# An eight-batch attention kernel: the last batch's scores are taken further ahead, and its last probabilities are turned a step sooner

## The chip, the core and the metric

The kernel runs on one core of a Trainium2 chip. The metric is device time in microseconds of one execution. Before the change it is 431.56 us, the median of three runs (429.86 to 432.5). PE is TensorE, DVE VectorE, ACT ScalarE, POOL GpSimd; SP issues transfers.

## What is computed

For each of 8 batches, 112 queries attend with 20 heads of 16 channels to 371 text tokens; four further prompt tokens have keys and values of their own, and their logits get half the cosine between the attended text and the prompt token. In the reference, cut to what matters:

```python
q = heads(hidden_states @ W_q)
k_t, v_t = heads(text_ehs @ W_k), heads(text_ehs @ W_v)
probs_t = softmax(einsum('bhsd,bhtd->bhst', q, k_t) * attn_scale)
text_out = einsum('bhst,bhtd->bhsd', probs_t, v_t)
attn_scores = einsum('bhsd,bhnd->bhsn', q, k_ip) * attn_scale
qsem = _l2norm(einsum('bhst,bte->bhse', probs_t, text_ehs))
sem = einsum('bhse,bne->bhsn', qsem, _l2norm(ip_ehs))
probs_ip = softmax(attn_scores + 0.5 * sem) * spatial_mask
out = (text_out + einsum('bhsn,bhnd->bhsd', probs_ip, v_ip)) @ W_out + b_out + residual
```

The length of the attended text is never formed from its 512 channels: with the Gram matrix G of the tokens it is the square root of p G p, so each head needs the product of its probabilities with G, the values and the prompt columns, and then a sum of that product times the probabilities.

## The kernel before

**Tiling.** The 20 heads of a batch are five groups of four. One step (b, g), counted from zero, handles one group of one batch; there are 40 steps. The four heads of a group lie on four bands of 32 partitions, so four small matmuls run side by side.

**A group's way.** `scores` (L672 to L689) multiplies masked queries and keys into one PSUM bank for each head. `probabilities` (L691 to L710) takes the maximum on DVE (L695), the exponential on ACT (L699), copies the four prompt logits (L701), and sends the probabilities by SP into `xg`, a ring of two buffers (L708). `transposed` (L712) turns `xg` on DVE into `xgT`, of which there are two (in the last batch in two halves). `multiplied` (L724) makes 48 matmuls, in 12 rounds of four with shrinking width (392 columns down to 40, 2592 over a head's twelve), into four banks (L737). Then the bank is evacuated: values and prompt products to `pvs` (L750, or L767), and the sum of product times probability either in one DVE instruction (L785, "junk") or, for some heads of the last steps, by `shared`: a copy on ACT (L768), a product on POOL (L772), a sum on ACT (L778). `placed` (L644) has POOL write the group's values into the right operand `u` (L651), chunk by chunk. `finish` (L802 to L924) ends a batch: squares and a maximum (L826, L828), a root and a table load on ACT (L843, L844), a reciprocal and the prompt softmax on DVE (L850 to L868), the prompt sums and the output projection on PE.

**Stores.** PSUM has eight banks: four `qd`, two `sc`, two `mm`; `bank(name, spare)` gives an `sc` or an `mm` bank. Probabilities have three buffers (`p`).

**Order.** On PE, SP and DVE, and from the second batch on ACT too, the instructions stand in the order in which the program calls them; in the last batch that holds for POOL too. So each engine is a queue written out by hand. In the main loop (L1187) a step issues the scores of the group two steps on: two of them at the first round and two at the seventh; the first two's probabilities follow at once, the others' after the step. At the third round the next group is turned. After the step come value copies, reductions, the placing of the next values, and in `between` (L1070) projections for later batches: keys, values, queries. `project_queries` (L315) runs in pieces; the last query product of batch 7 (L340) stands between (6,4) and (7,0).

**The last batch (L1260).** The same look-ahead of two steps: scores of group 2 in (7,0), of group 3 partly before and partly in (7,1), of group 4 in (7,2). The last third of the keys (`last_keys`, L550) stands between (7,0) and (7,1), in a `qd` bank, in two halves with two scores between. `finish` of batch 6 is threaded through the steps. The third transfer of group 4 is issued from ACT's queue (L710). Group 4 is turned in (7,3). `shared` takes three heads of groups 0, 1 and 2 and one of group 3. After the steps comes a tail in which batch 6 and batch 7 are finished.

Of the kernel before, what the change touches and what calls it, by code (L numbers as in the profile page):

```python
# [8 lines left out]
F32 = mybir.dt.float32  # L9
AF = mybir.ActivationFunctionType  # L10
# [10 lines left out]
def kernel(  # L21
# [292 lines left out]

    def project_queries(bs):  # L315
        n = len(bs)
        xT = work.tile([P, NC, 2 * S], F32, tag="xT", name=f"xT_{bs[0]}", bufs=1)
        qm = work.tile([P, NC, 2, 2 * S], F32, tag="qm", name=f"qm_{bs[0]}", bufs=2)

        qT = const.tile([P, NC, S], F32, tag="qT", name="qT") if bs[0] == 0 else None  # L320
        for j, b in enumerate(bs):
            queries[b] = (qT, qm, j)
        nc.gpsimd.memset(xT[REST:, FULL, :], 0.0)
        for i in range(NC):
            cn = min(P, C - i * P)
            if bs[0] == 0:

                ps = ps_qd.tile([P, 512], F32, tag="qd", name=f"ps_x_0_{i}")
            else:
                ps = bank(f"ps_x_{bs[0]}_{i}", spare=i > 0)  # L330
            for j, b in enumerate(bs):
                nc.tensor.transpose(
                    ps[:cn, j * S : (j + 1) * S], x_sb[:, b, i * P : i * P + cn], ident[:S, :S]
                )
            nc.scalar.copy(xT[:cn, i, : n * S], ps[:cn, : n * S])
            yield
        for i in range(NC):
            ps = bank(f"ps_q_{bs[0]}_{i}")
            for j in range(NC):
                nc.tensor.matmul(  # L340
                    ps[:, : n * S],
                    wq_sb[:, j, i * P : (i + 1) * P],
                    xT[:, j, : n * S],
                    start=(j == 0),
                    stop=(j == NC - 1),
                )

            for r in range(2 if i < FULL else 1):
                nc.vector.tensor_scalar_mul(  # L349
                    qm[:, i, r, : n * S], ps[:, : n * S], emask[:, r : r + 1]  # L350
                )
            if qT is not None:
                nc.scalar.copy(qT[:, i, :], ps[:, :S])
            yield
# [333 lines left out]
        )  # L688
        s["sc", g, a] = ps  # L689

    def probabilities(b, g, a):  # L691
# [3 lines left out]
        nc.vector.tensor_reduce(nmx, ps[:S, :TT], AX.X, ALU.max, negate=True)  # L695
        if ("p", g) not in s:
            s["p", g] = work.tile([S, GROUP, TT], F32, tag="p", name=f"p_{b}_{g}", bufs=3)
        p = s["p", g][:, a, :]
        nc.scalar.activation(p, ps[:S, :TT], AF.Exp, bias=nmx)  # L699
        if b > 0:  # L700
            nc.scalar.copy(s["ipl"][:, groups[g][a], :], ps[:S, TT:T])  # L701

        xg = x_ring[(b * NG + g) % NX]
        rows = xg[a * RG : a * RG + S // QN, :, :TT]
        if (b, g, a) == (B - 1, NG - 1, 1):
            s["third"] = rows, p
            return
        nc.sync.dma_start(rows, p)  # L708
        if "third" in s:
            nc.scalar.dma_start(*s.pop("third"))  # L710

    def transposed(b, g):  # L712

# [10 lines left out]
    def multiplied(b, g):  # L724
        s = st[b]
        xT = s.pop(("xT", g))
        banks = []
        for a in range(GROUP):

            if b == B - 1 and g % 2 and g < NG - 1:  # L730
                banks.append(bank(f"ps_qd_{b}_{g}_{a}", spare=a > 1))
            else:
                banks.append(ps_qd.tile([P, 512], F32, tag="qd", name=f"ps_qd_{b}_{g}_{a}"))
        for j in range(BLK):
            c, q = PLACE[j] if b > 0 else (j // QN, j % QN)
            for a in range(GROUP):
                nc.tensor.matmul(  # L737
                    banks[a][:S, j * RG : UW],
                    xT[a * RG : (a + 1) * RG, j, :S],
                    region(b, c)[a * RG : (a + 1) * RG, q, j * RG - c * P :],  # L740
                    start=(j == 0),
                    stop=(j == BLK - 1),
                )
            yield
        s["qd", g] = banks
# [6 lines left out]
    def shared(b, g, n):  # L752
# [17 lines left out]

        for a, _ in some:
            nc.gpsimd.tensor_tensor(prods[a], prods[a], p[:, a, :], ALU.mult)  # L772
            if (b, g) == (B - 1, LEAD) and a < n - 1:
                yield
        yield

        for a, (h, _) in some:
# [292 lines left out]
    def between(b, g):  # L1070
# [43 lines left out]
        if g == 4:  # L1114
            if b > 0 and new:
                run(("f", b - 1), None, 2)
            if nb < B - 1:
                run(("k", nb), None, 1)
            for bs in (first if b > 0 else []) + rest:
                run(("q", bs[0]), None)  # L1120

    prompts = normalised_prompts()
# [60 lines left out]
            load_x(5, B)  # L1183


    ctx.enter_context(tc.manual_schedule(engines=engines | {mybir.EngineType.Activation}))
    for n, (b, g) in enumerate(steps[:-NG]):  # L1187
        coming = steps[n + LEAD]
# [17 lines left out]
        for a in (0, 1):  # L1206
            probabilities(*coming, a)
        if n == len(steps) - NG - 1:
            sums = shared(b, g, GROUP // 2)
            next(sums)  # L1210
# [36 lines left out]
    b = B - 1  # L1247
    before = ("f", b - 1)

    def coming(g, heads):  # L1250

        for a in heads:
            if g == 1:
                ps = ps_qd.tile([P, 512], F32, tag="qd", name=f"ps_s_{b}_{g + LEAD}_{a}")
            else:
                ps = bank(f"ps_s_{b}_{g + LEAD}_{a}", spare=a > 1)
            scores(b, g + LEAD, a, ps=ps)
            probabilities(b, g + LEAD, a)

    for g in range(NG):  # L1260
        if g == 1:
            keys3 = last_keys(b, ps_qd.tile([P, 512], F32, tag="qd", name=f"ps_k_{b}_{FULL}"))
            next(keys3)
            coming(g, (3, 0))
            next(keys3)
            run(before, lambda: finish(b - 1, bd=bd[:, 0]))
        places = {0: {0: (2, 3), 1: (0, 1)}, 1: {0: (1, 2)}, 2: {0: (3, 0), 1: (1, 2)}}.get(g, {})
        for j, _ in enumerate(multiplied(b, g)):
            coming(g, places.get(j, ()))
            if g == NG - 2 and j in (QN - 1, 2 * QN - 1):  # L1270
                next(sums)
                placed(b, g + 1, (j // QN,))
            if j != 2:
                continue
            if g < LEAD:
                drain(sums)
            if g + 1 < NG:
                transposed(b, g + 1)
            if g == 2:
                run(before, None)  # L1280
            if g == 3:
                run(before, None)
        ahead = sums
        if g < NG - 1:

            n = GROUP - 1 if g <= LEAD else 1
            sums = shared(b, g, n)
            next(sums)
            reduced(b, g, n)
            if g <= LEAD:  # L1290
                value_sums(b, g, n)
            if g == NG - 2:
                placed(b, g + 1, (NT - 1,))
                next(ahead)
            else:
                placed(b, g + 1)
            if g != LEAD:
                next(sums)
        if g == 0:
            own_channels(bd)  # L1300
            with_bias(b)
            run(("f", b - 2), None)
        if g == 2:
            run(before, None, 2)
            drain(ahead)
            nc.scalar.preload_act_table(AF.Sqrt)
        if g == 3:
            drain(ahead)
            drain(sums)
            value_sums(b, g, n)  # L1310

            first = finish(b, (0, FULL * HC), bd=bd[:, 1])
            for _ in range(3):
                next(first)
    value_sums(b, g)
    next(first)
    late = projected_prompts(bd[:, 1])
    run(before, None)
    next(late)
# [62 lines left out]
```

## Time and profile before

| What | us |
|---|---|
| median of three runs | 431.56 |
| the profiled execution | 432.11 |
| its span, first to last instruction | 430.1 |
| PE busy (share) | 418.8 (97%) |
| DVE busy (share) | 326.8 (76%) |
| ACT busy (share) | 190.1 (44%) |
| POOL busy (share) | 111.6 (26%) |
| granted TensorE clock, mean | 1.000 |

The page gives busy time for each engine and the chain of work that ended last. The timeline lists instructions of one engine that follow each other as one row: start, time, engine, line, operation, out<-in, shape, count, and in brackets how long the engine had been idle and what ended that. PEld is the load of the stationary operand, which overlaps PE. In the timeline the four matmuls of a round overlap, so a row's time is longer than the work's share of it. Idle time of an engine that nobody waits for costs nothing.

### The profile page before, as it was taken

The page shows a single profiled execution, that of the slowest core. Times are in us where ns is not written, and L with a number is a line of the kernel's source. Part 1 is how long each engine was busy: PE and PEld are TensorE (multiplying, and loading weights), DVE is VectorE, ACT ScalarE, POOL GpSimd, SP SyncE. Part 2 cuts the span into 40 slices and gives each one's busy share as a digit, 9 for nine tenths or more (in the row PEclk, how much of TensorE's full clock was granted, in tenths as well). Part 3 has the DMA queues.
Part 4 walks back from the last instruction along what each step waited for, and adds up shares of the span by engine and source line. Part 5 has one row for each costly group of instructions (what it writes and reads, how often), then busy time and mean ns, then how long its engine had stood idle before and what let it go on. Part 6 is the DMA issues. An engine that isn't in the chain of part 4 may idle for free. (4 is left out here: it accounts for less than half of the span.)

```text
span 430.1 us, 13979 instructions
## 1 busy us (share of the span) xinstructions
PE 418.8 (97%) x5521; PEld 327.3 (76%) x5521; DVE 326.8 (76%) x670; ACT 190.1 (44%) x662; POOL 111.6 (26%) x276
## 2 busy tenths in 40 slices
PE   8999999989999999999999999999999999999976
PEld 7867768878777877888777977789777887776773
DVE  4038569787887878887897978888878877878784
ACT  2344342345334353435334353344533463346783
POOL 5310101112061212421251111511142120527340
PEclk9999999999999999999999999999999999999999
DMA  8677665687646966576646946477656446553300
GB/s 234 201 192 209 141 167 161 160 200 148 161 127 145 202 155 168 140 164 147 168 121 139 203 117 175 123 163 153 168 139 160 132 109 185 139 127 111 93 2 27
DMA packets 57630, 64.26 MB, mean 149 GB/s; under 512 B 18448, under 2 KB 51592, under 8 KB 57566
## 3 DMA queue, kind: packets, MB, share of 16 engines
q1 hardware_dynamic: 56808, 62.26, 58.2%
q10 hardware_dynamic: 758, 1.13, 0.9%
q8 instruction: 43, 0.70, 0.7%
q14 instruction: 21, 0.17, 0.1%
HBM read 18.67 MB, written 5.32 MB: 56 GB/s over the span
## 5 line engine op out<-in xcount | busy, mean ns | idle before, releaser
L737 PE MATMUL ps_qd<-u,xgT 32*112 32x328 f32 (+11 forms) x3840 | 220.1, 353 | 1.3 <-DVE xgT L718 1.3
L737 PEld LDWEIGHTS ps_qd<-u,xgT 32*112 32x112 f32 x3840 | 187.0, 172 | 34.5 <-issue 10.9
L718 DVE STREAM_TRANSPOSE xgT<-xg 128x1536 f32<-128x1536 f32 (+1 forms) x45 | 119.1, 2667 | 11.4 <-DMA xg<-p 10.8
L699 ACT ACTIVATE p<-ps_s,nmx 112x371 f32<-112x371 f32 x160 | 86.9, 580 | 84.4 <-DVE nmx L695 59.7
L695 DVE TENSOR_REDUCE nmx<-ps_s 112x1 f32<-112x371 f32 x160 | 77.7, 528 | 42.1 <-PE ps_s L682 40.0
L785 DVE CUSTOM_DVE_ANT_0 junk<-ps_qd,p 112x371 f32<-112x371 f32 x148 | 80.2, 542 | 15.5 <-ACT kT L536 0.5
L682 PE MATMUL ps_s<-kT,qm 32*112 32x375 f32 (+1 forms) x320 | 66.8, 485 | 0.7 <-ACT shared L768 0.7
L651 POOL COPY u<-vr 128x64 f32<-128x64 f32 x120 | 26.0, 237 | 149.5 <-PE ps_qd L737 100.2
L574 PE MATMUL ps_v<-wv_sb,ctxT 128*128 128x384 f32 (+1 forms) x192 | 63.6, 480 | 0.0
L574 PEld LDWEIGHTS ps_v<-wv_sb,ctxT 128*128 128x128 f32 x192 | 35.2, 190 | 19.7
L540 PE MATMUL ps_k<-ctxT,wk_sb 128*128 128x371 f32 x136 | 46.3, 483 | 0.2 <-DVE ctxT L421 0.2
L750 ACT COPY pvs<-ps_qd 112x21 f32<-112x21 f32 x150 | 15.9, 188 | 64.0 <-PE ps_qd L737 63.1
L540 PEld LDWEIGHTS ps_k<-ctxT,wk_sb 128*128 128x128 f32 x136 | 24.9, 190 | 15.2 <-POOL ct L138 0.5
L682 PEld LDWEIGHTS ps_s<-kT,qm 32*112 32x112 f32 x320 | 26.8, 170 | 6.8 <-ACT kT L547 2.1
L498 PE MATMUL ps_g<-ctxT 128*32 128x375 f32 (+11 forms) x672 | 30.4, 333 | 0.0
L498 PEld LDWEIGHTS ps_g<-ctxT 128*32 128x32 f32 x672 | 27.7, 110 | 2.0
L701 ACT COPY ipl<-ps_s 112x4 f32<-112x4 f32 x140 | 23.4, 167 | 0.0
L349 DVE TENSOR_SCALAR qm<-ps_q,emask 128x224 f32<-128x224 f32 (+1 forms) x25 | 9.1, 399 | 17.6 <-PE ps_q L340 17.5
L400 DVE STREAM_TRANSPOSE ctxT<-ct 128x512 f32<-128x512 f32 x18 | 20.0, 1109 | 1.9 <-DMA ct<-in_ctx_dram 1.9
L581 ACT COPY vext<-ps_v 128x384 f32<-128x384 f32 (+1 forms) x24 | 11.3, 471 | 21.2 <-PE ps_v L574 21.2
L471 POOL TENSOR_TENSOR ug<-ug,half 128x128 f32<-128x128 f32 (+1 forms) x24 | 10.4, 446 | 32.0 <-ACT ug L470 32.0
L928 POOL TENSOR_TENSOR wv<-vip,w 112x1280 f32<-112x1280 f32 x6 | 14.8, 2465 | 14.2 <-DVE w L868 14.2
(167 smaller groups left out, 320.7 us busy)
## 6 DMA issues: line engine op xcount, KB each, us to landing
xg<-p SPq DMA_DIRECT2D x159, 162.3 KB
u<-ug SPq DMA_DIRECT2D x124, 99.0 KB
ct<-in_ctx_dram SPq DMA_DIRECT2D x24, 176.0 KB
vr<-vd SPq DMA_DIRECT2D x32, 120.0 KB
vip<-vipd SPq DMA_DIRECT2D x6, 560.0 KB
vd<-vext SPq DMA_DIRECT2D x7, 320.0 KB
vd<-vext SPq DMA_DIRECT2D x7, 160.0 KB
out_dram<-ob SPq DMA_DIRECT2D x8, 140.0 KB
```

The costliest lines, as they stand in the source:

```text
L400: nc.vector.transpose(ctxT[:, :, c * P : (c + 1) * P].rearrange("p e (j i) -> p j e i", i=RG), ct[:, some, :].rearrange("p j (k e) -> p j ...
L498: nc.tensor.matmul(ps[c][q * RG : (q + 1) * RG, j * RG - c * P : T - c * P], ctxT[:, e, j * RG : (j + 1) * RG], ctxT[:, e, j * RG : T], st ...
L540: nc.tensor.matmul(ps[:, :TT], wk_sb[:, e, i * P : (i + 1) * P], s["ctxT"][:, e, :TT], start=(e == 0), stop=(e == NE - 1),)
L574: nc.tensor.matmul(ps[:, :w], ctxT[:, e, c * P : (c + 1) * P], wv_sb[:, e, :w], start=(e == 0), stop=(e == NE - 1),)
L651: nc.gpsimd.tensor_copy(v, dealt(b, c, s["vr"][:, c * QN : (c + 1) * QN, g, :]))
L682: nc.tensor.matmul(ps[:S, :w], qm[a * RG : (a + 1) * RG, i, r, j * S : (j + 1) * S], s["kT"][a * RG : (a + 1) * RG, i, :w], start=True, st ...
L695: nc.vector.tensor_reduce(nmx, ps[:S, :TT], AX.X, ALU.max, negate=True)
L699: nc.scalar.activation(p, ps[:S, :TT], AF.Exp, bias=nmx)
L701: nc.scalar.copy(s["ipl"][:, groups[g][a], :], ps[:S, TT:T])
L718: nc.vector.transpose(xT[:, j : j + n].rearrange("p j (k q) -> p q j k", q=QN), xg[:, :, j * RG : (j + n) * RG].rearrange("p q (j k) -> p ...
L737: nc.tensor.matmul(banks[a][:S, j * RG : UW], xT[a * RG : (a + 1) * RG, j, :S], region(b, c)[a * RG : (a + 1) * RG, q, j * RG - c * P :], ...
L785: nc.vector.tensor_tensor_reduce(out=junk, in0=ps[:S, :TT], in1=s["p", g][:, a, :], scale=1.0, scalar=0.0, op0=ALU.mult, op1=ALU.add, accu ...
```

## The change

From step (6,3) on, scores are issued half a group further ahead. `ahead` (new) gives for each step which scores come at its first round, which of them get an `mm` bank and have their transfer held back (`hold`, `sent`), and which come at the seventh round. (6,3) issues all four of (7,0) and two of (7,1); (6,4) the other two of (7,1) and all of (7,2); (7,0) all of group 3; (7,1) all of group 4, at its third and fourth rounds; (7,2) none. Held transfers are issued after the turn that frees their ring buffer. The probabilities of groups 1 and 3 of the last batch get other homes (`home`): a free context buffer and the value weights, which have had their last use. The last query product of batch 7 moves from between (6,4) and (7,0) to between (7,0) and (7,1), behind the last keys, which stand there in one piece and in an `mm` bank. Groups 2, 3 and 4 are turned one step sooner, at the ends of (7,0), (7,1) and (7,2). `shared` takes three, three, two and no heads of groups 0 to 3, and its last sums on ACT come a step later. All of group 4's transfers are on SP. In the tail the weights of batch 6 (L863 to L868) come after the first root's inputs of batch 7.

```diff
@@ project_queries
-            ps = bank(f"ps_q_{bs[0]}_{i}")
+            if end and i == FULL:
+                ps = ps_qd.tile([P, 512], F32, tag="qd", name=f"ps_q_{bs[0]}_{i}")
+            else:
+                ps = bank(f"ps_q_{bs[0]}_{i}")
@@ probabilities
-        if (b, g, a) == (B - 1, NG - 1, 1):
-            s["third"] = rows, p
-            return
-        nc.sync.dma_start(rows, p)
-        if "third" in s:
-            nc.scalar.dma_start(*s.pop("third"))
+        if not hold:
+            sent(b, g, a)
@@ between
-            for bs in (first if b > 0 else []) + rest:
+            for bs in (first if b > 0 else []) + (rest if b < B - 2 else []):
@@ the main loop
+    def ahead(n):
+        c, d = steps[n + LEAD : n + LEAD + 2]
+        if steps[n] == (B - 2, NG - 2):
+            todo = ((c, 2, 3), (c, 0, 1), (d, 2, 3))
+        elif steps[n] == (B - 2, NG - 1):
+            todo = ((c, 0, 1), (d, 2, 3), (d, 0, 1))
+        else:
+            todo = ((c, 2, 3), (c,), (c, 0, 1))
+        return [[(t[0], a) for a in t[1:]] for t in todo]
...
-            for a in {0: (2, 3), 6: (0, 1)}.get(j, ()):
-                scores(*coming, a)
-                if j == 0:
-                    probabilities(*coming, a)
+            if j == 0:
+                for c, a in now:
+                    scores(*c, a)
+                    probabilities(*c, a)
+                for c, a in more:
+                    scores(*c, a, ps=bank(f"ps_s_{c[0]}_{c[1]}_{a}"))
+                    probabilities(*c, a, hold=True)
+            if j == 6:
+                for c, a in then:
+                    scores(*c, a)
             if j == 2:
...
                 transposed(*steps[n + 1])
+                for c, a in more:
+                    sent(*c, a)
@@ the last batch
         if g == 1:
-            keys3 = last_keys(b, ps_qd.tile([P, 512], F32, tag="qd", name=f"ps_k_{b}_{FULL}"))
+            keys3 = last_keys(b, bank(f"ps_k_{b}_{FULL}"))
             next(keys3)
-            coming(g, (3, 0))
             next(keys3)
-            run(before, lambda: finish(b - 1, bd=bd[:, 0]))
+            run(("q", b), None)
+            drain(late)
...
+            if g == 0 and j < 2:
+                for a in ((2, 3), (0, 1))[j]:
+                    coming(NG - 2, a, bank(f"ps_s_{b}_{NG - 2}_{a}", spare=a > 1))
+            if g == 0 and j == 2:
+                transposed(b, 1)
+                for a in range(GROUP):
+                    sent(b, NG - 2, a)
+            if g == 1 and j in (2, 3):
+                for a in ((3, 2), (1, 0))[j - 2]:
+                    ps = ps_qd.tile([P, 512], F32, tag="qd", name=f"ps_s_{b}_{NG - 1}_{a}")
+                    coming(NG - 1, a, ps)
+            if g == 1 and j == 4:
+                run(before, lambda: finish(b - 1, bd=bd[:, 0]))
...
+        n = (3, 3, 2, 0)[g]
+        late, sums = sums, shared(b, g, n) if n else iter(())
+        next(sums, None)
+        reduced(b, g, n)
+        value_sums(b, g, n)
+        if g == LEAD:
+            run(before, None, 2)
+        if 0 < g + 1 < NG - 1:
+            transposed(b, g + 2)
+        placed(b, g + 1, range(NT) if g == 0 else (NT - 1,))
+        next(sums, None)
+        if g > 0:
+            drain(late)
```

More of the change, by code (lines that the diff above doesn't have):

```diff
@@ L316, in project_queries @@
         n = len(bs)
+        end = bs[0] == B - 1
         xT = work.tile([P, NC, 2 * S], F32, tag="xT", name=f"xT_{bs[0]}", bufs=1)
@@ L689, in scores, with home, probabilities @@
         s["sc", g, a] = ps
-    def probabilities(b, g, a):
+    def home(b, g):
+        if b == B - 1 and g == 1:
+            t = io.tile([P, NT, E], F32, tag="ct", name=f"p_{b}_{g}").rearrange("p c e -> p (c e)")
+        elif b == B - 1 and g == 3:
+            t = wv_sb.rearrange("p e f -> p (e f)")
+        else:
+            return work.tile([S, GROUP, TT], F32, tag="p", name=f"p_{b}_{g}", bufs=3)
+        return t[:S, : GROUP * TT].rearrange("p (a t) -> p a t", t=TT)
+    def probabilities(b, g, a, hold=False):
         s = st[b]
@@ L728, in multiplied @@
         for a in range(GROUP):
-            if b == B - 1 and g % 2 and g < NG - 1:
+            if b == B - 1 and g % 2:
                 banks.append(bank(f"ps_qd_{b}_{g}_{a}", spare=a > 1))
@@ L772, in shared @@
             nc.gpsimd.tensor_tensor(prods[a], prods[a], p[:, a, :], ALU.mult)
-            if (b, g) == (B - 1, LEAD) and a < n - 1:
-                yield
         yield
@@ L1183, in load_rest @@
             load_x(5, B)
+    def ahead(n):
[4 more added lines that the diff above has]
+            todo = ((c, 0, 1), (d, 2, 3), (d, 0, 1))
+        else:
+            todo = ((c, 2, 3), (c,), (c, 0, 1))
+        return [[(t[0], a) for a in t[1:]] for t in todo]
     ctx.enter_context(tc.manual_schedule(engines=engines | {mybir.EngineType.Activation}))
     for n, (b, g) in enumerate(steps[:-NG]):
-        coming = steps[n + LEAD]
+        now, more, then = ahead(n)
         for j, _ in enumerate(multiplied(b, g)):
-            for a in {0: (2, 3), 6: (0, 1)}.get(j, ()):
-                scores(*coming, a)
-                if j == 0:
-                    probabilities(*coming, a)
+            if j == 0:
[8 more added lines that the diff above has]
+                    scores(*c, a)
             if j == 2:
@@ L1205 @@
             run(("f", b - 1), None)
-        for a in (0, 1):
-            probabilities(*coming, a)
+        for c, a in then:
+            probabilities(*c, a)
         if n == len(steps) - NG - 1:
@@ L1248, with coming @@
     before = ("f", b - 1)
[L1250 to L1258, printed above, removed]
+    def coming(g, a, ps):
+        scores(b, g, a, ps=ps)
+        probabilities(b, g, a, hold=g == NG - 2)
     for g in range(NG):
@@ L1283 @@
[L1283 to L1298, printed above, removed]
+            if g == 0 and j < 2:
+                for a in ((2, 3), (0, 1))[j]:
+                    coming(NG - 2, a, bank(f"ps_s_{b}_{NG - 2}_{a}", spare=a > 1))
@@ new lines @@
+            if g == 0 and j == 2:
[8 more added lines that the diff above has]
+                run(before, lambda: finish(b - 1, bd=bd[:, 0]))
+            if 0 < g < NG - 1 and j in (QN - 1, 2 * QN - 1):
+                placed(b, g + 1, (j // QN,))
@@ L1299 @@
+        if g == NG - 1:
+            break
+        n = (3, 3, 2, 0)[g]
[11 more added lines that the diff above has]
+            drain(late)
         if g == 0:
@@ L1302 @@
             run(("f", b - 2), None)
+        if g == 1:
+            run(before, None)
         if g == 2:
-            run(before, None, 2)
-            drain(ahead)
             nc.scalar.preload_act_table(AF.Sqrt)
         if g == 3:
-            drain(ahead)
-            drain(sums)
-            value_sums(b, g, n)
             first = finish(b, (0, FULL * HC), bd=bd[:, 1])
-            for _ in range(3):
+            for _ in range(2):
                 next(first)
+            run(before, None)
+            next(first)
+            next(first)
     value_sums(b, g)
-    next(first)
     late = projected_prompts(bd[:, 1])
```

22 lines of the change are left out of this document (4 added, 18 removed).

## The prediction

> **What bounds the kernel now.** Steps are named (batch, group), counted from zero; times of the new kernel are estimates on the clock of the old trace. I read the page's engine totals first, then the chain that ended last, then PE's waits over the last 60 us, then the timeline from 364 us on, where the diff acts; before step (6,3) the instruction order is the same on every engine.
>
> ```profile
> PE 418.8 (97%) x5521; PEld 327.3 (76%) x5521; DVE 326.8 (76%) x670; ACT 190.1 (44%) x662; POOL 111.6 (26%) x276
> ```
>
> ```profile
> 404.70 4.64 DMA xg<-p
> ...
> 409.46 2.97 DVE xgT L718 x2
> ```
>
> ```profile
> PE ps_qd L737 <- DVE xgT L718: 1.3, 1, 1.3
> ...
> PE ps_s L682 <- ACT shared L768: 0.7, 1, 0.7
> ```
>
> Over the whole span PE is busy 97%, but the chain at the end is not PE's: a probability transfer lands 4.64 us after issue, VectorE then turns group 4 (L718), and the rest of the tail follows. The waits list shows PE two holes in the last batch, before (7,4) and inside (7,2), 2.0 us together; more lie around the key products, whose rows follow below. So at most some 3.5 us can be had by filling holes and starting the turn earlier; the number of matmuls, maxima, exponentials and transfers doesn't change.
>
> **Part 1: six scores instead of four in (6,3) and in (6,4).** The rows show (6,3) from its end on, (6,4), and in the last row (7,4), which holds no scores; names on a row are out<-in, xN the count.
>
> ```profile
> 372.39 2.76 PE L540 MATMUL ps_k<-ctxT,wk_sb 128*128 128x371 f32 x8
> ...
> 374.68 0.14 PEld L941 LDWEIGHTS ps_a<-ident,attn 112*128 112x128 f32 x1
> ...
> 375.31 0.55 DVE L785 CUSTOM_DVE_ANT_0 junk<-ps_qd,p 112x371 f32<-112x371 f32 x1
> ...
> 376.04 1.22 PE L737 MATMUL ps_qd<-u,xgT 32*112 32x392 f32 x10
> ...
> 376.15 0.58 DVE L349 TENSOR_SCALAR qm<-ps_q,emask 128x112 f32<-128x112 f32 x2 [0.29 <-PE ps_q L340]
> ...
> 378.54 2.97 DVE L718 STREAM_TRANSPOSE xgT<-xg 128x768 f32<-128x768 f32 x2
> ...
> 381.35 0.95 DVE L695 TENSOR_REDUCE nmx<-ps_s 112x1 f32<-112x371 f32 x2
> ...
> 381.41 1.87 PE L953 MATMUL ps_o<-wo_sb,aT 128*112 128x320 f32 x6
> ...
> 411.19 5.05 PE L737 MATMUL ps_qd<-u,xgT 32*112 32x392 f32 x96 [1.29 <-DVE xgT L718]
> ```
>
> A step with four scores takes PE 381.41-376.04 = 5.37, one with none 5.05 (last row): 0.08 per score, as four run side by side. Two more cost PE 0.16, so (6,4) could start at 376.20. VectorE is dearer: two more maxima (0.95) stand before the four reductions of (6,3), whose last ended at 375.86 (375.31+0.55) and now ends at 376.82. The fourth bank of (6,4) waits for it, and behind it on VectorE come the masked queries (0.58, to 377.45); the second pair of early scores, moved here, needs those queries. Bounds of the stall: 0, and the 0.95 of the maxima. I take 0.35, nearer to 0, since three of the four first products and two scores run meanwhile. So (6,4) ends at 376.20+5.37+0.16+0.35 = 382.08, 0.67 late.
>
> **The start of (7,0).** Before, the query product stood here and covered the evacuation of (6,4).
>
> ```profile
> 381.88 0.57 ACT L699 ACTIVATE p<-ps_s,nmx 112x371 f32<-112x371 f32 x1
> ...
> 382.85 0.91 PEld L340 LDWEIGHTS ps_q<-xT,wq_sb 128*128 128x128 f32 x6
> ...
> 382.89 0.87 ACT L768 COPY shared<-ps_qd 112x371 f32<-112x371 f32 x2
> ...
> 383.86 1.22 PE L737 MATMUL ps_qd<-u,xgT 32*112 32x392 f32 x10
> ...
> 384.62 0.48 PE L682 MATMUL ps_s<-kT,qm 32*112 32x375 f32 x2
> ...
> 385.45 1.89 DVE L695 TENSOR_REDUCE nmx<-ps_s 112x1 f32<-112x371 f32 x4 [1.15 <-PE ps_s L682]
> ...
> 386.08 0.57 ACT L699 ACTIVATE p<-ps_s,nmx 112x371 f32<-112x371 f32 x1 [2.32 <-POOL shared L772]
> ...
> 387.26 3.02 DVE L718 STREAM_TRANSPOSE xgT<-xg 128x768 f32<-128x768 f32 x2
> ...
> 388.06 0.21 ACT L701 COPY ipl<-ps_s 112x4 f32<-112x4 f32 x1
> ```
>
> In (6,4) VectorE goes on from 377.45 with four maxima (385.45 to 387.26, so 1.81 each four) and a turn (378.54 to 381.35, so 2.81) to 382.07. The next exponential starts 0.63 after its maximum does (386.08-385.45): 382.70. From there to the end of the second "shared" copy passed 382.89+0.87-381.88 = 1.88, so two banks of (7,0) come free at 384.58, PE at 384.65. PE is done with L953 (1.44, worked out below) by 383.5 and waits 1.1; the query product (383.86-382.85 = 1.01) no longer covers this, it has moved behind (7,0). So (7,0) starts 0.8 late. Bounds: without any wait PE gets there at 376.20+5.37+0.16 = 381.73 and L953, which takes 382.85-381.41 = 1.44, so at 383.17, 0.7 early; and 1.9 late, twice 0.95.
>
> **Part 2: keys, queries, and group 4's scores in (7,1).**
>
> ```profile
> 389.91 1.51 PE L556 MATMUL ps_k<-ctxT,wk_sb 128*128 128x371 f32 x4 [0.62 <-ACT shared L768]
> ...
> 393.61 1.21 PE L737 MATMUL ps_qd<-u,xgT 32*112 32x392 f32 x9
> ```
>
> Before, (7,0) ended at 383.86+5.37 = 389.23 and (7,1) began at 393.61: keys in two halves, two scores between, each behind ScalarE's copies (0.62 ahead of the first half). Now the keys have a bank of the other pool, free since the exponentials of group 3, and run in one piece: 2.29 for eight such products (374.68-372.39), then queries 1.01. (7,0) ends at 384.65+5.37 = 390.02, (7,1) starts at 393.32: 0.29 early. The lateness is paid back by the holes that were there. Beneath it VectorE turns (7,2) right behind (7,0)'s last reduction; it is some 0.8 late against before and free by 394.5, masked queries by 394.9. Group 4's first score stands three rounds into (7,1), 1080 of 2592 columns of 5.05: 395.42, so it needn't wait, by 0.5.
> (7,1) ends at 393.32+5.37 = 398.69. But (7,2) takes the banks of group 4's scores. From a first score to the end of the fourth logits copy took 388.27-384.62 = 3.65, so the last bank is free at 399.1: (7,2) gets going 0.4 late and ends, with no scores in it, at 399.1+5.05 = 404.15. Before it ended at 411.19-1.29-5.05 = 404.85. PE has won 0.7 here, and (7,3) and (7,4) follow without the hole of 1.29.
>
> **Part 3: the turn and the tail.** VectorE, not the transfer, now sets when group 4 is turned.
>
> ```profile
> 367.47 0.30 DVE L868 SCALAR_TENSOR_TENSOR w<-ex,sm_sb,rx 112x80 f32<-112x80 f32 x1
> ...
> 369.79 1.73 SPq L708 DMA_DIRECT2D xg<-p  x2
> ...
> 405.98 0.53 DVE L785 CUSTOM_DVE_ANT_0 junk<-ps_qd,p 112x371 f32<-112x371 f32 x1
> ...
> 407.63 0.24 DVE L856 TENSOR_TENSOR fu<-fu,mx 112x80 f32<-112x80 f32 x1
> ...
> 412.29 0.17 DVE L864 TENSOR_REDUCE sx<-ex 112x20 f32<-112x80 f32 x1
> ...
> 412.87 0.97 POOL L772 TENSOR_TENSOR shared<-shared,p 112x371 f32<-112x371 f32 x1 [1.24 <-ACT shared L768]
> 412.88 1.06 DVE L868 SCALAR_TENSOR_TENSOR w<-ex,sm_sb,rx 112x80 f32<-112x80 f32 x1
> ...
> 413.19 0.51 ACT L778 ACTIVATE shared<-shared 112x371 f32<-112x371 f32 x1
> ...
> 414.55 0.54 DVE L785 CUSTOM_DVE_ANT_0 junk<-ps_qd,p 112x371 f32<-112x371 f32 x1
> ...
> 415.25 0.55 DVE L785 CUSTOM_DVE_ANT_0 junk<-ps_qd,p 112x371 f32<-112x371 f32 x1
> ...
> 416.04 0.19 DVE L826 SCALAR_TENSOR_TENSOR z<-pvs 112x16 f32<-112x16 f32 x1 [0.24 <-ACT pvs L750]
> ...
> 416.72 0.25 DVE L850 RECIPROCAL rn<-rn 112x16 f32<-112x16 f32 x1
> ...
> 418.43 0.26 ACT L880 COPY wT<-ps_wT 80x112 f32<-80x112 f32 x1
> ```
>
> The last transfer of group 4 is issued by about 400.0 (exponential 399.1, one issue 1.73/2) and lands, at 4.64, near 404.7. VectorE has two reductions of (7,2) now, 415.25-414.55 = 0.70 apart, from about 404.25, then the normalisation, 407.63+0.24-405.98 = 1.89 from the last reduction's start to the end of L856. The turn starts at 404.25+0.70+1.89 = 406.84, 2.6 sooner than at 409.46. Behind it stand four reductions instead of three: 412.29-409.46 = 2.83 for the turn, three steps of 0.70, and 416.04-415.25 = 0.79 from the last one to z (L826) give 412.56 against 416.04, 3.5 sooner. Two things are given back. ScalarE sums two products (0.51 each) between the value copies, which end with z's start, and the root: 413.58. VectorE does the sums and weights of batch 6 (L864 to L868: 412.88-412.29 = 0.59 and L868's 0.30) ahead of the second reciprocal: z and its two followers end by 413.1, so that comes at about 414.0, against 416.72. The four value copies of (7,4) now follow the exponential: at most 0.21 each, as L701 at 388.06, and overlapped; I take 0.3. So wT, 1.71 behind that reciprocal before (418.43), comes at 414.0+1.71+0.3 = 416.0, 2.4 sooner. If L868 takes 1.06 again, as it did beside the POOL product at 412.87, it is 0.76 less, 1.65. GpSimd's L834 now starts in that same place; I take the middle, 2.0. From wT on the order is as before, so the end moves by as much.
>
> [...]
>
> **Sum.** Profiled execution 432.11 (its span and 2.0 around it), which is 0.55 over the median of the runs, 431.56. 432.11-2.0 = 430.1; on the median, 429.6. ScalarE's own transfer issue at the end goes; nothing waited for it.
>
> **Rivals.**
> A: PE pays the whole lateness of VectorE, 0.95 at (6,4) and 1.9 at (7,0). For it: PE executes in order, and in (6,4) a score that waits holds the products behind it. Against: a bank at a time comes free. (7,0) starts 1.1 later than forecast and all behind it too: gain 0.9, 430.7; with the stall at group 4's banks doubled, no gain.
> B, slower: the value rows of batch 7 come too late.
>
> ```profile
> 376.05 3.19 SPq L599 DMA_DIRECT2D vr<-vd  x4
> ...
> 381.62 0.59 POOL L651 COPY u<-vr 128x64 f32<-128x64 f32 x3 [7.25 <-DMA xg<-p]
> ```
>
> SP now has two more probability transfers ahead of them (0.87 each, row above), so they are issued by 381.0 instead of 379.24. At the 2.38 seen from there to POOL's copy, that starts at 383.4 and hides, by about 1 us. Each us beyond delays (7,0) and all behind it; the gain is gone when they land 3.0 later, and at twice the 4.64 of the chain's transfer it ends near 435.
> C: no stalls in (6,4) and (7,0), as the lanes of PE absorb them: 1.5 more gained (0.7 early against 0.8 late), 428.1. For it: rows of four run side by side. Against: two banks are ScalarE's, after VectorE.
>
> **How the numbers follow.** Forecast 0.62 (gain of 1.2 to 3, 428.5 to 430.4), A 0.20, B 0.08, C 0.10. The range 427.6 to 432.4 holds the first, A and C with the spread of the runs, and leaves B out. About 1% is what a measurement of this kernel can tell from no change, 4.3 us; only C with luck gets below 427.2 and only B above 435.9: faster 0.06, same 0.89, slower 0.05.
>
> **What would show it.** (6,4) ending near 382.1 and (7,0) starting near 384.6 behind L768 copies; no gap between keys and queries; no PE wait for xgT at (7,4); the last turn starting near 406.8 behind L856, not behind a transfer. Wrong if PE idles in (7,1) before group 4's scores, if POOL's first copy for (7,0) waits for vr past 384.6, or if the gap from z to wT grows by more than 2.

## The result, and the profile after

The changed kernel takes 433.26 us (median of 20 runs, 430.74 to 436.55). The kernel before, on the same chip, takes 430.77 (20 runs, 429.82 to 433.26). The ratio is 1.0048 with a 95% interval of 1.0025 to 1.0071: slower by half a per cent, where 429.6 was forecast. The profiled execution took 434.03 with a span of 432.2 (before: 432.11 and 430.1).

From the page of the changed kernel: the engine totals, and the clock that TensorE was granted in 40 slices, in tenths of full speed.

```profile
PE 422.2 (98%) x5521; PEld 331.1 (77%) x5521; DVE 327.5 (76%) x674; ACT 188.9 (44%) x656; POOL 110.0 (25%) x274
...
PEclk9999999999999999999999999999999999999988
```

PE is busier than before, 422.2 against 418.8, with the same 5521 matmuls, and the last two slices of the clock read 8. The longest wait of PE over the last 130 us:

```profile
PE ps_wT L883 <- DVE w L877: 1.4, 1, 1.4
```

The columns are the time waited in all, how often, and the longest. The hole of 1.3 for xgT has shrunk to 0.58 (the row of (7,4) below) and the one of 0.7 for ScalarE's copies is gone. A new one of 1.4 stands at the transposition of w. (w holds the prompt weights of batch 6; PE transposes them into the bank ps_wT, and ScalarE copies that to wT, which the last products of the batch read.) The timeline of the tail shows where (7,4) ends, 409.81+4.92 = 414.73, and what follows:

```profile
409.81 4.92 PE L748 MATMUL ps_qd<-u,xgT 32*112 32x392 f32 x96 [0.58 <-DVE xgT L729]
...
416.12 0.27 PE L883 MATMUL ps_wT<-ident,w 112*80 112x112 f32 x1 [1.39 <-DVE w L877]
...
417.68 0.27 ACT L889 COPY wT<-ps_wT 80x112 f32<-80x112 f32 x1
...
421.77 3.06 PE L917 MATMUL ps_o<-wo_sb,aT 128*112 128x320 f32 x6
...
428.84 0.49 DVE L1057 TENSOR_TENSOR ob<-ps_o,bd 112x320 f32<-112x320 f32 x1 [3.48 <-PE ps_o L1053]
```

The same transposition and the same two last steps of the kernel before:

```profile
416.17 0.29 PE L874 MATMUL ps_wT<-ident,w 112*80 112x112 f32 x1
...
420.78 1.87 PE L908 MATMUL ps_o<-wo_sb,aT 128*112 128x320 f32 x6
...
426.72 0.49 DVE L1048 TENSOR_TENSOR ob<-ps_o,bd 112x320 f32<-112x320 f32 x1 [2.38 <-PE ps_o L1044]
```

The hole is there because only one side moved: (7,4) ends 1.51 sooner (414.73, before 411.19+5.05 = 416.24), but w is transposed only 0.05 sooner (416.12, before 416.17). The copy of wT comes at 417.68, 0.75 sooner than the 418.43 of before. The last output tile (ob) comes 2.12 later. So 2.87 us are lost between wT and the end, a stretch whose instructions the change does not touch. Six products of the projection take 3.06 there instead of 1.87.

The granted clock says why. In the changed kernel it reads full speed for 409.60 us (7.79 to 417.39) and half for the next 6.83. The rows tell it in windows of 3.413 us, counted from where its record begins: the fall lies 120 of them behind that, the rise 122. That the unit is one window and not two is an estimate from the mean clocks below, of which 0.996 fits one. The columns are stretch, length, PE busy, instructions, granted clock, DMA share, GB/s. First the changed kernel, then the kernel before:

```profile
413.98:417.39 3.41, 2.02 (x41) 1.00 0.00 0
417.39:420.80 3.41, 3.22 (x15) 0.50 0.00 0
420.80:424.22 3.42, 3.42 (x7) 0.50 0.00 0
```

```profile
416.89:420.30 3.41, 2.42 (x20) 1.00 0.00 0
420.30:423.71 3.41, 3.33 (x17) 1.00 0.00 0
```

In the changed kernel PE is busy 2.02 of one window, and for the two windows behind it the clock is 0.50: PE shows as busy for 6.64 of these 6.83 us, at half speed. In the kernel before the clock stays at 1.00. The 20 runs follow the clock too: mean granted clock 0.999 or 1.000 in 430.74, 430.96, 431.07 and 431.46; 0.996 in 431.18 to 433.53; 0.991 in 432.71 to 434.18; 0.983 in 436.33 and 436.55. One window of 3.41 at half clock is 3.41 x 0.5 / 432 = 0.004 of the mean, so 0.996 is one such window, 0.991 two and 0.983 four. Even the four runs at 0.999 or 1.000 are no faster than the kernel before (430.77), so the clock is not all that is missing from the forecast of 429.6.

### The profile page after: what moved, and what is told of

Read it like the earlier page. It is cut to its first block, busy times and chain, and to the rows that moved or that the text cites. A ratio compares the mean times of both kernels' runs of the same rounds, so it can differ in the third digit from the quotient of the medians.

```text
span 432.2 us, 13976 instructions
## 1 busy us (share of the span) xinstructions
PE 422.2 (98%) x5521; PEld 331.1 (77%) x5521; DVE 327.5 (76%) x674; ACT 188.9 (44%) x656; POOL 110.0 (25%) x274
## 4 chain that ended last, share of the span: by engine, by line
PE 88%; DMA 4%; DVE 4%; ACT 2%; SPq 1%; issue 1%; DVEq 0%; ACTq 0%
PE ps_qd L748 42%; PE ps_v L578 13%; PE ps_k L544 9%; PE ps_g L502 7%; PE ps_s L686 5%; PE ps_q L344 3%; PE ps_o L962 2%; DMA xg<-p 2%; DMA vipx<-vipd 2%; DVE xgT L729 1%; PE ps_g L458 1%; PE ps_o L917 1%; DVE junk L794 1%; DMA ct<-in_ctx_dram 1%; PE ps_k L560 1%
## 5 line engine op out<-in xcount | busy, mean ns | idle before, releaser
L712 ACT ACTIVATE p<-ps_s,nmx 112x371 f32<-112x371 f32 x156 | 84.9, 582 | 78.1 <-DVE nmx L709 62.0
L794 DVE CUSTOM_DVE_ANT_0 junk<-ps_qd,p 112x371 f32<-112x371 f32 x146 | 79.2, 542 | 17.7 <-PE ps_qd L748 1.6
L686 PE MATMUL ps_s<-kT,qm 32*112 32x375 f32 (+1 forms) x320 | 64.9, 483 | 0.1
```

Source lines behind the costliest of these rows:

```text
L686: nc.tensor.matmul(ps[:S, :w], qm[a * RG : (a + 1) * RG, i, r, j * S : (j + 1) * S], s["kT"][a * RG : (a + 1) * RG, i, :w], start=True, st ...
L712: nc.scalar.activation(s["p", g][:, a, :], ps[:S, :TT], AF.Exp, bias=nmx)
L794: nc.vector.tensor_tensor_reduce(out=junk, in0=ps[:S, :TT], in1=s["p", g][:, a, :], scale=1.0, scalar=0.0, op0=ALU.mult, op1=ALU.add, accu ...
```

## The experiments

Two theories. **G**: the tail of the changed kernel gives PE a hole (the 1.39 ahead of L883) followed by few and small products, the granted clock falls, and that is the loss. **Q**: the loss comes from queues, that is from the late start of (7,0), from VectorE's steps slowed beside GpSimd, and from the late root of ScalarE; the clock is a companion. Where the expectations speak of the gate, the granted clock is meant.

### The kernel before once more

No edit.

> The kernel before once more, for the spread of its executions and their granted clocks. Theory G (the clock falls in the tail of the changed kernel because PE ends (7,4) sooner and then idles 1.4 us ahead of the next transpose, and this costs some 3 us) expects a mean clock of 1.000 in nearly all executions here, none below 0.995, and a span of about 428.5 to 430.1. Theory Q (the loss is in the hand-written queues: the wait at the start of (7,0), the slow VectorE steps ahead of the last turn, the late root; the clock is incidental) expects no tie of time and clock: executions with a lower clock here too, at the same share as in the changed kernel.

431.35 (12 runs, 430.13 to 433.36) against 431.95 of the shared runs of before; ratio 0.9983 (0.9957 to 1.0009). The mean clock was 0.995 or more in all twelve, as G expected. But of the 35 shared runs of this same kernel 6 showed 0.991 or 0.992 and took 433.61 to 435.34, and of the 32 that were shared by the later experiments 4 showed 0.992 and took 434.31 to 435.11, so it is not immune. What follows: the fall is not the changed kernel's alone, but there it is the rule (1.000 or 0.999 in only 4 of 20).

### The hole filled

```
             ps = bank(f"ps_wT_{b}")
+            if b == B - 2:
+                warm(ps, 5)
```

Five dummy products of the identity stand ahead of w's transposition, on the changed kernel.

> The changed kernel with five more dummy products of 128x128 on PE, in the bank of the first transposed weights, so that PE is busy between the end of (7,4) and that transpose. Theory G expects no PE idle over 0.5 us there, a clock of 1.000 in most executions, a span near 428.8 and a time near 430.8, some 2.5 under the changed kernel's median. Theory Q expects the time of the changed kernel, 433, or a little more, since the transpose waits for the last dummy.

430.84 (12 runs, 430.3 to 432.05), ratio to before 0.9975 (0.9952 to 0.9998), mean clock 0.998 to 1.000 in every run. The timeline and the window around it:

```profile
414.08 1.38 PE L439 MATMUL ps_wT<-ident 128*128 128x128 f32 x10
...
417.11 0.27 ACT L891 COPY wT<-ps_wT 80x112 f32<-80x112 f32 x1
...
425.77 0.49 DVE L1059 TENSOR_TENSOR ob<-ps_o,bd 112x320 f32<-112x320 f32 x1 [2.37 <-PE ps_o L1055]
```

```profile
414.25:417.67 3.42, 3.02 (x23) 1.00 0.00 0
```

More work made the kernel faster: 2.4 us below the changed kernel's 433.26 by the medians, and by the ratios to the kernel before, each on its own chip, 0.9975 against 1.0048. From wT to the last tile it takes 425.77-417.11 = 8.66, against 428.84-417.68 = 11.16 with the half clock: 2.50 of clock. Nothing was done for the queues. G holds, and Q cannot give this.

### The query product back between (6,4) and (7,0)

```
-            if end and i == FULL:
-                ps = ps_qd.tile([P, 512], F32, tag="qd", ...)
-            else:
-                ps = bank(f"ps_q_{bs[0]}_{i}")
+            ps = bank(f"ps_q_{bs[0]}_{i}")
...
-            for bs in (first if b > 0 else []) + (rest if b < B - 2 else []):
+            for bs in (first if b > 0 else []) + rest:
...
-            run(("q", b), None)
```

> The changed kernel with one part undone: the last query product stands between (6,4) and (7,0) again. It should cover the evacuation wait there. Expected where the clock doesn't decide: (7,0) starts no later, (7,1) starts some 0.9 us sooner behind the keys, and the last turn on VectorE starts sooner by as much. Theory Q expects the time 0.9 under the changed kernel's. Theory G expects the same shift in the trace up to the last root, but a time that follows the clock: executions at 1.000 near 430.0, those with the gate closed near 432.5.

433.08 (12 runs, 431.16 to 434.15), ratio 1.0019 (0.9992 to 1.0046), with the mean clock at 0.991 or 0.996 in 11 of 12 runs. No gain shows. First the changed kernel, then the experiment; the whole of the experiment runs 0.69 later (its first query product of the batch starts at 376.80, that of the changed kernel at 376.11):

```profile
390.86 2.45 PE L560 MATMUL ps_k<-ctxT,wk_sb 128*128 128x371 f32 x7
...
393.46 0.82 PE L344 MATMUL ps_q<-xT,wq_sb 128*128 128x112 f32 x6
...
393.66 0.47 ACT L567 COPY kT<-ps_k 128x371 f32<-128x371 f32 x1 [1.32 <-PE ps_k L560]
...
396.12 0.48 PE L686 MATMUL ps_s<-kT,qm 32*112 32x375 f32 x2
```

```profile
391.54 1.83 PE L556 MATMUL ps_k<-ctxT,wk_sb 128*128 128x371 f32 x5
...
394.34 0.47 ACT L563 COPY kT<-ps_k 128x371 f32<-128x371 f32 x1 [1.32 <-PE ps_k L556]
...
396.77 0.58 PE L682 MATMUL ps_s<-kT,qm 32*112 32x375 f32 x3
```

Less the 0.69, the keys start at 390.85 in the experiment, the copy of kT at 393.65 and group 4's first score at 396.08: the same to 0.04 as in the changed kernel. The product costs nothing in either place. Ahead of (7,0) it lies beside the evacuation of (6,4): (7,0) starts 0.65 later, and PE no longer waits in its first round. Behind the keys it lies beside ScalarE's copy of kT: without it there, (7,1) starts 0.66 sooner, near the 0.9 that was expected, but then waits 0.36 for that copy, as its banks include that of the keys. My count of what its move cost was wrong, and the late start of (7,0) was not the loss.

### Two orders at once

VectorE's first step of the normalisation stands ahead of the reductions of (7,2), and ScalarE's two sums of group 2 ahead of the value copies of group 3. The rest is the changed kernel.

```
         next(sums, None)
+        if g == LEAD:
+            run(before, None)
+        if g == 3:
+            drain(late)
         reduced(b, g, n)
         value_sums(b, g, n)
         if g == LEAD:
-            run(before, None, 2)
+            run(before, None)
```

> The changed kernel with two orders changed in the last batch: batch 6's reciprocal and normalisation go ahead of the two reductions of (7,2) on VectorE, so away from POOL's product; and the two sums of group 2 on ACT go ahead of the value copies of group 3. The two slow steps (0.90 and 0.62 in the changed kernel) should take about 0.25 each and the last turn start about 1.1 us sooner, and the root not wait 0.8 for ACT's sums: the transposed weights are copied 1.5 to 2 us sooner. Theory Q expects the time 1.5 to 2 under the changed kernel's, near 431.5. Theory G expects that at a clock of 1.000 (near 429), and less idle of PE ahead of the first transpose of the tail, so the gate closed in fewer executions: a median near 429.5 to 431.

429.16 (12 runs, 428.7 to 431.47), ratio 0.9944 (0.9919 to 0.997): faster than both kernels, 0.3 under G's range and 2.3 under the 431.5 of Q. First the rows of the changed kernel that it acts on, then its own:

```profile
404.60 0.55 DVE L794 CUSTOM_DVE_ANT_0 junk<-ps_qd,p 112x371 f32<-112x371 f32 x1 [1.32 <-PE ps_qd L748]
...
406.18 1.90 POOL L783 TENSOR_TENSOR shared<-shared,p 112x371 f32<-112x371 f32 x2 [1.17 <-ACT shared L779]
406.35 0.90 DVE L862 SCALAR_TENSOR_TENSOR fu<-fu,ipl 112x80 f32<-112x80 f32 x1
...
407.55 0.62 DVE L865 TENSOR_TENSOR fu<-fu,mx 112x80 f32<-112x80 f32 x1
...
408.10 2.96 DVE L729 STREAM_TRANSPOSE xgT<-xg 128x768 f32<-128x768 f32 x2
...
413.76 0.19 DVE L835 SCALAR_TENSOR_TENSOR z<-pvs 112x16 f32<-112x16 f32 x1 [0.24 <-ACT pvs L761]
...
414.76 0.17 DVE L837 TENSOR_TENSOR rn<-ss,z 112x16 f32<-112x16 f32 x1 [0.81 <-ACT shared L787]
...
414.97 0.21 ACT L852 ACTIVATE rn<-rn 112x16 f32<-112x16 f32 x1 [0.24 <-DVE rn L837]
```

```profile
405.97 3.02 DVE L729 STREAM_TRANSPOSE xgT<-xg 128x768 f32<-128x768 f32 x2
...
413.29 0.26 PE L883 MATMUL ps_wT<-ident,w 112*80 112x112 f32 x1 [0.22 <-DVE w L877]
...
414.86 0.27 ACT L889 COPY wT<-ps_wT 80x112 f32<-80x112 f32 x1
...
423.52 0.49 DVE L1057 TENSOR_TENSOR ob<-ps_o,bd 112x320 f32<-112x320 f32 x1 [2.38 <-PE ps_o L1053]
```

In the changed kernel L862 and L865 lie beside GpSimd's products (406.18 to 408.08) and take 0.90 and 0.62 instead of 0.24 each; the sum L837 then waits 0.81 for ScalarE. Here the last turn starts 1.37 sooner and wT comes 2.06 sooner, counted from the first query product of the batch (376.11 and 375.35), and PE waits 0.22 for w instead of 1.39. From wT to the last tile it takes 8.66, as with the filled hole. Two kinds of cure, one of the queues and one of the clock, are in this kernel together, so the next two experiments take them one at a time.

### Each order by itself

Of the edit above, the lines for g == LEAD alone, and then the lines for g == 3 alone.

> The changed kernel with only the first of e4_order's two orders: one step of the normalisation stands ahead of the reductions of (7,2), away from the POOL products. Last turn sooner by about 1.1 to 1.4 against the changed kernel (L862 and L865 at 0.24 each instead of 0.90 and 0.62). The root still waits 0.8 for ScalarE's sums, and TensorE waits at w for about as long as before (1.4), since what stands ahead and behind moves alike. G: the gate still falls in many executions, clock 0.99 in some, median 430.5 to 432.5, with the ones at 1.00 near 429.6. Q: 1.2 below the changed kernel in all: 431.6 to 432.2.

430.32 (12 runs, 429.71 to 432.9), ratio to before 0.9979 (0.9953 to 1.0005).

> The changed kernel with only the second of e4_order's two orders: ScalarE's two sums of group 3 ahead of the value copies, so that the root needn't wait for them. Root and w 0.8 sooner, the last turn unchanged at its late place (VectorE beside POOL). TensorE's wait at w falls from 1.4 to about 0.6. G: with the hole cut to 0.6 the clock stays at 0.998 or more in most executions; so about 3 us of half clock and 0.8 of wait go: 429.8 to 430.6. Q: only the 0.8 of the wait goes: 432.2 to 432.8.

430.87 (12 runs, 430.26 to 432.7), ratio 0.9976 (0.9952 to 1.0000); before was 431.58 for both. First the normalisation alone, then the sums alone:

```profile
404.12 0.24 DVE L862 SCALAR_TENSOR_TENSOR fu<-fu,ipl 112x80 f32<-112x80 f32 x1
...
414.08 0.27 PE L883 MATMUL ps_wT<-ident,w 112*80 112x112 f32 x1 [0.99 <-DVE w L877]
...
415.64 0.27 ACT L889 COPY wT<-ps_wT 80x112 f32<-80x112 f32 x1
```

```profile
414.30 0.27 PE L883 MATMUL ps_wT<-ident,w 112*80 112x112 f32 x1 [0.62 <-DVE w L877]
...
415.87 0.27 ACT L889 COPY wT<-ps_wT 80x112 f32<-80x112 f32 x1
```

Counted from the first query product (375.35 and 375.04), wT comes at 40.29 and at 40.83, against 41.57 in the changed kernel and 39.51 with both: 1.28 and 0.74 by themselves, 2.06 together. The sizes add up. (The hole of the first was expected to stay at 1.4; it is 0.99.) Both medians are below what Q expected, and within 0.3 of G's ranges (0.2 under the one, 0.3 over the other). The mean clock was 0.991 or 0.992 in only 3 of 12 runs of either kernel (432.12 to 432.9 and 432.47 to 432.7), among them both profiled ones, and 0.998 or more in the rest. With a shorter hole (0.99 and 0.62 instead of 1.39) the fall is rarer (the changed kernel shows 0.992 or less in 13 of 20); it is not excluded.

### The kernel before with a hole

The three dummy products that the kernel before has in its tail, behind ps_wT, are taken out.

```
-            if b == B - 2:
-                warm(ps, 3)
```

> The kernel before, without the three dummy products of L435 that stand behind ps_wT in the last batch's tail. G (the granted clock falls when TensorE's tail is too sparse): the same fall is made in the old kernel, without any part of the change: granted clock below 0.997 in at least half of the executions, windows at 0.50 behind 417, L908 at 3 instead of 1.87, and 432.5 to 434. If the clock stays at 1.00 and the time at 430.8 to 431.4, a hole of the 0.9 us that these products fill is too small for it, and G stands only for the 1.4 us of the changed kernel. Q (the loss is lateness of the queues, the clock a companion): 430.8 to 431.4, whatever the clock does.

432.8 (12 runs, 430.94 to 437.17), ratio 1.0024 (0.999 to 1.0058). The mean clock was 0.995 or less in 9 of 12 runs, and 0.998 in the other three; of the 32 shared runs of the kernel before, 7 show 0.995 or less. The windows of its profiled execution:

```profile
415.20:418.61 3.41, 2.12 (x17) 1.00 0.00 0
418.61:422.02 3.41, 3.41 (x9) 0.50 0.00 0
422.02:425.44 3.42, 3.42 (x13) 0.50 0.11 32
```

The same fall, after the same kind of window, without any part of the change; and the median goes up by 1.2, where Q expected 430.8 to 431.4, although work was taken out. In this execution the stretch from wT to the last tile takes 11.36 instead of 8.29. The interval of the ratio still includes 1, so the size of the loss in the median is not settled by it. That taking work out of the tail makes the fall the rule is.

### Both orders, and the hole filled

The two orders and the five dummy products together.

> The changed kernel with both orders of e4_order (normalisation of group 2 one step sooner, ScalarE's sums of group 3 ahead of the value copies) and the five dummy products of e2_filled ahead of ps_wT. In e4_order TensorE waits only 0.2 for w, so the five products (1.38 for ten records in e2_filled) stand mostly in the way of the transposition of w. G: clock at 0.998 and more in every execution (e4_order had one of 0.994 at 431.47), but 0.3 to 0.9 slower than e4_order's 429.16 in the fast ones: 429.4 to 430.0. Q: the same 429.4 to 430.0 and the clock no steadier than in e4_order.

428.85 (9 runs, 428.36 to 429.8), ratio 0.9923 (0.9897 to 0.995), clock 0.998 to 1.000 in all. Both theories expected the dummies to cost 0.3 to 0.9 here. They cost nothing:

```profile
413.94 0.26 PE L885 MATMUL ps_wT<-ident,w 112*80 112x112 f32 x1
...
414.16 0.26 ACT L869 ACTIVATE ex<-fu 112x64 f32<-112x64 f32 x1 [0.78 <-DVE fu L865]
...
414.59 0.27 ACT L891 COPY wT<-ps_wT 80x112 f32<-80x112 f32 x1
```

Counted from the first query product (375.08), w's transposition starts at 38.86, where the kernel with the orders alone has it at 37.94. Yet the copy of wT stands at 39.51 in both: it is queued on ScalarE behind the exponential of batch 7's first sixteen heads (L869), so PE had 0.9 to spare. This is the lowest median here, 0.8% below the kernel before; from the two orders alone (0.9944) it is not told apart, since the intervals overlap.

## Why the prediction was wrong

**The step that failed**: "From wT on the order is as before, so the end moves by as much." The order was as before, but not the clock. From wT to the last tile the kernel before takes 426.72-418.43 = 8.29, the changed kernel 11.16, and the kernels with the clock kept 8.66. The kernel with the query product back has the same hole (1.38) and kept the clock in its profiled execution, and it takes 8.66 too. So 2.50 of the loss are the half clock. The other 0.37 lies with VectorE, here by the rows of the filled hole: its first reduction of (7,4) starts 0.07 ahead of wT instead of 0.22, the last two follow at 0.69 each instead of 0.58, and so z_last comes 3.08 behind wT instead of 2.71. PE then waits 0.82 for w_last, where its wait at that place was 0.46 before. Why the reductions are further apart stays open. I had treated each hole that goes as a gain and never asked what the holes that are left do to PE's speed behind them. The prediction has no term for the granted clock at all, and no rival that it could have been. The gain at wT was itself only half of the forecast, for the reasons below, and so there is none to see even where the clock stays.

**The early part** came out near the forecast in time, but with a wrong price in it, and its errors were paid back. (6,3) starts 0.21 later in this execution than in that of before (367.24 and 367.03), and so each forecast is moved by 0.21 here:

```profile
367.24 0.93 PE L748 MATMUL ps_qd<-u,xgT 32*112 32x392 f32 x8
...
373.23 2.76 PE L544 MATMUL ps_k<-ctxT,wk_sb 128*128 128x371 f32 x8
...
376.88 1.04 PE L748 MATMUL ps_qd<-u,xgT 32*112 32x392 f32 x8
...
382.86 1.87 PE L962 MATMUL ps_o<-wo_sb,aT 128*112 128x320 f32 x6
...
384.65 0.27 PEld L748 LDWEIGHTS ps_qd<-u,xgT 32*112 32x112 f32 x2 [0.45 <-POOL u L655]
```

(6,4) ended at 382.86 instead of 382.29. No stall behind VectorE is to be seen in it. (6,3), in which none was forecast, takes 373.23-367.24 = 5.99 instead of 5.36, and (6,4) 382.86-376.88 = 5.98 instead of 5.37, with PE busy throughout. So two more scores cost 0.62 in each step where the sum has 0.16, and the price of 0.08 per score was the term that was wrong; the 0.35 that was put for a stall made up for part of it. (7,0) started at 384.65, near the 384.6 that was named, but not behind the "shared" copies, which run from 384.60 to 385.47; the row names GpSimd's value copies (384.02 to 384.61), but in the kernel with both orders these end 0.28 ahead of the start, with the same wait. The first round then took 1.39 instead of 0.76, with 0.29 of it a wait for VectorE's reduction. So the start was met by luck, while the stretch from the end of (6,4) to the keys was right: 8.00, forecast 7.94. The keys started at 390.86 instead of 390.23, 0.6 late, and queries follow them without a gap, as forecast. Group 4's first score came at 396.12 instead of 395.63. By the first reduction of (7,2), forecast at 404.46 and measured at 404.60, the lateness was gone: the 0.4 that I had given to group 4's banks did not come, and a step without scores is shorter (4.92 for (7,4), 5.05 before). Rival A's size came at (6,4), but from the scores themselves, and its 1.1 more at (7,0) did not. Rival B did not happen: the value copies came 0.4 later than forecast and still ended ahead of (7,0). Rival C's gain did not come: (6,4) had no stall, but (7,0) waited.

**The last turn** does start behind L865 and not behind a transfer, as forecast, but at 408.10 instead of 407.05. 0.14 came with (7,2), 0.66 and 0.38 are L862 and L865 beside GpSimd, and 0.13 was won between. So PE still waits 0.58 for xgT ahead of (7,4), where no wait was forecast. I had priced the normalisation from a row where nothing ran beside it (1.89 in all), in the same paragraph in which 1.06 was weighed for L868 for just that reason. On that later step the middle price, 0.68, was too high: L877 took 0.43.

**The root** was forecast with 1.02 behind z for ScalarE's two sums; it was 414.97-413.76 = 1.21. That was the right mechanism at nearly the right size, but it could have been avoided: the sums had no need to stand behind the value copies, and moving them brought wT 0.74 sooner.

**The sum.** At wT the forecast gain was 2.0; measured it is 0.75, or 0.96 with the 0.21. With both orders mended, wT stands 2.06 sooner than in the changed kernel, so 3.0 ahead of the kernel before, more than was forecast. The forecast gain was there to be had; half of it came (0.96 of 2.0). Then 0.75 sooner at wT, 0.37 and 2.50 later behind it make the last tile 2.12 later.

**What stays open.** Which window brings the clock down is not settled. Four windows were followed by half clock, with PE busy 2.02, 2.12, 2.32 and 2.46 of 3.41. The last two are those of the normalisation alone and of the sums alone:

```profile
412.32:415.73 3.41, 2.32 (x38) 1.00 0.00 0
```

```profile
413.52:416.93 3.41, 2.46 (x23) 1.00 0.00 0
```

Others with as little were not followed by a fall: the 2.42 of the kernel before, shown above, and these of the query product back, of the kernel before once more, and of the two orders at once:

```profile
413.51:416.93 3.42, 2.04 (x60) 1.00 0.00 0
```

```profile
409.28:412.70 3.42, 1.97 (x36) 1.00 0.02 5
```

```profile
421.37:424.78 3.41, 2.11 (x8) 1.00 0.13 42
```

So PE's busy time alone does not decide, nor does the number of instructions (17 to 41 where the clock fell, 8 to 60 where it stayed), nor the longest hole (0.62 was followed by a fall; the kernel before has 0.99 ahead of L891 and kept its clock). Nor does the same kernel do the same each time: the 20 runs of the changed kernel have means from 0.983 to 1.000. The fall comes 41.28 us behind the first query product of the batch in the changed kernel (417.39-376.11), 40.38 with the normalisation alone and 41.89 with the sums alone, so the windows lie differently against the program in these executions. Whether that decides was not shown: no run here moved them on purpose.

## What to carry to other kernels

Look at the granted clock of the tail before counting on a gain there: here dense work of TensorE ended 1.5 us sooner, what it waited for next did not, and a fall of the clock behind that hole cost 2.5 us. A hole that cannot be closed by order can be filled with dummy products, as long as the next engine in the chain is not yet ready for what follows them; here five of them were worth 2.4 us alone and cost nothing on top of the better order. When a VectorE step is moved, price it by what GpSimd does at its new place (0.90 for L862 beside its product, 0.24 without), and when a chain comes sooner, look at what is queued ahead of it on the other engines: two reorderings of one step each brought the weights 1.28 and 0.74 us sooner. And price a score by itself where four of them follow one another: two more took 0.62 of PE here, not 0.16.

## What was unexpected of the hardware

- The clock fell behind windows in which PE was at work: 2.02 to 2.46 us of work in 3.41 us were followed by two windows at 0.50, in four profiled executions of four kernels. With 3.02 in the window (the filled hole) it stayed at 1.00, but so it did behind windows of 1.97 to 2.42.
- Busy time hides it. PE reads 3.42 of 3.42 busy at half clock, and the changed kernel's page shows PE busier than before (422.2 against 418.8) for the same matmuls.
- VectorE's L862 (two inputs, 112x80) takes 0.24 by itself and 0.90 beside GpSimd's product, and L865 0.24 and 0.62: the lengthening is 0.66 and 0.38. What in the hardware lengthens them was not shown.
